# A scan of 256 steps: one tangent per stream's step, 64 features per product, and the other products laid between the steps

## The chip, the cores and the metric

The kernel runs on one core of one Trainium2 chip. The metric is the device time of one launch in microseconds (us); lower is better. Engines are called as the profile calls them: PE is the matrix engine, PEld its loading of weights, ACT, DVE and POOL are the other three computing engines, SP issues transfers.

## The reference, cut to what matters

The whole kernel is a stack of eight layers over 8 sequences of 256 tokens with 128 features (four attention-like layers and four feed-forward layers with experts). The change touches only the first layer, a recurrence over time with 16 heads of 8 features and 64 states each:

```python
x = tokens * rsqrt(mean(tokens**2) + 1e-4) * norm_w      # then (B, T, 16, 8)
a_t = tanh(a)                                            # (16, 64, 64)
def step(state, x_t):                                    # state (B, 16, 64)
    state = tanh(einsum('bhs,hst->bht', state, a_t) + einsum('bhd,hds->bhs', x_t, b))
    mixed = einsum('bhs,hsd->bhd', state, c) + skip[None] * x_t
    return (state, mixed)
_, outs = scan(step, zeros, moveaxis(x, 1, 0))           # 256 steps, one after the other
return tokens + outs @ w_out.T + b_out
```

Every step needs the state of the step before it. All arithmetic is in 32-bit floats.

## The kernel before

**What comes around the scan.** `tile_post_ln_blocks` first runs `l0_attn`: it loads the weights, normalizes the tokens in four groups, transposes them (L128), writes the scaled features `xd` (L205) and `xnT` (L209), runs the scan, and then multiplies by `w_out` (L280) and adds the residual. Only then do the experts of the first feed-forward layer (`experts`, L306, L301) and everything after it start; they need the scan's result. The order of instructions on each engine is chosen when the program is built, by a scheduler that goes by its own estimates of durations; a manual dependency can hold an order. A helper called `behind` adds such a dependency without a semaphore: it only says that one instruction is to stand after another.

**How states are laid out.** The 16 heads are two streams (`h` = 0, 1) of 8 heads. A stream has four stacks `k`; a stack holds two heads, one in partitions 0 to 63 and one in 64 to 127. In the free dimension of a state tile stand, for each step, the four stacks with two column groups `e` of 8 batches: 4 x 2 x 8 = 64 columns. Where the head of the upper 64 partitions is meant (`e` = 1), the lower partitions hold zeros in those columns, and the other way round; so one product with all 128 partitions as rows serves two heads. Which heads form a stack changes from even to odd steps, so that the product's two halves land in the right partitions for the next step.

**One step of one stream before.** Eight products (L239): for two pairs of stacks `s` and four column groups of 32 features `c`, each with 128 rows, 32 columns of weights from `a_sb` and 16 moving columns of the last state. They add to a bank of PSUM that already holds the input products. Then two tangents (L248), one for each half of the partitions, write the 64 x 32 results that are not zero to the state tile; the zeros are set once at the start (L188) and stay.

**A block.** `TB` is 16 steps. Before a block's steps, 64 input products (L224, 32 columns of weights, 128 moving columns: 8 steps of one parity) fill the two banks of the block; the pool has four banks, so that the next block's products may run while this block's steps go on. After a block, 16 output products (L259, 32 columns of weights, 128 moving columns) and four instructions on DVE (L269, L270) write `outsT`. Where these 64 and 16 products stand among the steps is decided by the scheduler: in the program before, the input products come in bunches of 2 to 28 in the first steps of a block, with none in most steps, and the output products in pairs around the block's end.

**A product in 32-bit floats** shows as two records of PE in the profile (8160 records for the 4080 products of L239), each with its own record on PEld. The array can be split by columns: products of 32 columns of weights use one of four column groups and run beside each other, products of 64 columns use one of two halves.

Of the kernel before, what the change touches and what calls it, by code (L numbers as in the profile page):

```python
# [42 lines left out]
def tile_post_ln_blocks(ctx: ExitStack, tc: tile.TileContext, I, out: bass.AP):  # L43
# [10 lines left out]
    def bank(pool):  # L54
        return pool.tile([P, 512], F32, tag=pool.name, name=pool.name)
# [103 lines left out]
    def l0_attn(x):  # L159

        TB = 16
        cols = [slice(32 * c, 32 * c + 32) for c in range(4)]
        low, high = slice(0, 64), slice(64, 128)
        with ExitStack() as es:
            wp = es.enter_context(tc.tile_pool(name="l0w", bufs=1))
            wk = es.enter_context(tc.tile_pool(name="l0k", bufs=2))
            a_sb = load(wp, "L0_a")  # L170
            b_sb = load(wp, "L0_b")
            c_sb = load(wp, "L0_c")
            normw = load(wp, "L0_norm_w")
# [36 lines left out]

            ps_m = es.enter_context(tc.tile_pool(name="ps_s", bufs=4, space=bass.MemoryType.PSUM))
            prev = [None, None]
            for blk in range(T // TB):
                ts = slice(blk * TB // 2, (blk + 1) * TB // 2)
                st = [states[h][blk % 2] for h in range(2)]
                us = [
                    bank(ps_m).rearrange("p (s u t e b) -> p s u t e b", s=2, u=2, t=TB // 2, e=2)
                    for h in range(2)
                ]
                for u in range(2):  # L220
                    for h in range(2):
                        for s in range(2):
                            for c in range(4):
                                PE.matmul(  # L224
                                    us[h][cols[c], s, u].rearrange("p t e b -> p t (e b)"),
                                    lhsT=b_sb[:, u, 4 * h + 2 * s + c // 2, 32 * (c % 2) : 32 * (c % 2) + 32],
                                    rhs=xd[:, ts, u, :, :].rearrange("p t e b -> p t (e b)"),
                                    start=(u == 0 and s == 0),
                                    stop=False,
                                    skip_group_check=True,  # L230
                                )
                for t in range(TB):
                    v, u = t // 2, t % 2
                    for h in range(2):
                        if prev[h] is not None:
                            for s in range(2):
                                for c in range(4):
                                    k = 2 * s + c // 2
                                    PE.matmul(  # L239
                                        us[h][cols[c], s, u, v].rearrange("p e b -> p (e b)"),  # L240
                                        lhsT=a_sb[:, u, 4 * h + k, 32 * (c % 2) : 32 * (c % 2) + 32],
                                        rhs=prev[h][:, k].rearrange("p e b -> p (e b)"),
                                        start=False,
                                        stop=(t == TB - 1),
                                        skip_group_check=True,
                                    )
                        for e, half in enumerate((low, high)):
                            S.activation(  # L248
                                st[h][half, v, u, :, e, :].rearrange("p (s k) b -> p s k b", s=2),
                                us[h][half, :, u, v, :, :],  # L250
                                AF.Tanh,
                            )
                        prev[h] = st[h][:, v, u]

                pm = bank(lanes[blk % 2].ps)[:, : TB * 2 * B].rearrange("p (u t e b) -> p u t e b", u=2, t=TB // 2, e=2)
                for u in range(2):
                    for k in range(2):
                        for q, c in enumerate(cols):
                            PE.matmul(  # L259
                                pm[c, u].rearrange("p t e b -> p t (e b)"),  # L260
                                lhsT=c_sb[:, u, 2 * q + k, :],
                                rhs=st[q // 2][:, :, u, 2 * (q % 2) + k].rearrange("p t e b -> p t (e b)"),
                                start=(u == 0 and k == 0),
                                stop=(u == 1 and k == 1),
                                skip_group_check=True,
                            )
                for u in range(2):
                    o = outsT[:, :, blk * TB : (blk + 1) * TB].rearrange("p b (t u) -> p t u b", u=2)[:, :, u]
                    V.scalar_tensor_tensor(o, xnT[:, ts, u], skip, pm[:, u, :, 0], ALU.mult, ALU.add)  # L269
                    V.tensor_tensor(o, pm[:, u, :, 1], o, ALU.add)  # L270

            for g in range(NG):
                xb = wk.tile([P, 4, D], F32, tag="sq", name="xb")
                V.scalar_tensor_tensor(
                    xb, x[g], 2.0, bout.unsqueeze(1).to_broadcast([P, 4, D]), ALU.mult, ALU.add
                )
                ps = quarters(bank(lanes[g % 2].ps))
                for j in range(4):
                    i = 4 * g + j
                    PE.matmul(  # L280
                        ps[:, j, :],
                        lhsT=outsT[:, i // 2, (i % 2) * P : (i % 2) * P + P],
                        rhs=woT,
                        start=True,
                        stop=True,
                    )
                V.tensor_tensor(xb, ps, xb, ALU.add)
                mixed(lanes[g % 2], g, xb)
# [1097 lines left out]
```

## Time and profile before

| | |
|---|---|
| median of 5 runs | 2153.83 us (2146.22 to 2169.53) |
| the profiled execution | 2153.46 us, of which the span of instructions is 2151.7 us |
| PE busy in the span | 1804.5 us (84%) |
| ACT busy | 949.4 us (44%) |
| first input product (L224) | 25.48 us from the span's start |
| last tangent (L248) | ends at 307.8 us |
| granted TensorE clock from 25.48 to 308.10 us | 0.69 of full speed on average |
| granted clock from 310 to 900 us | 0.96 |

Read it as a chain of stages. The scan takes 282 us of 2151.7 us, one eighth, and nothing else of weight runs beside it. In the profile's rows a form such as "128*32 128x16" is a product with 128 rows and 32 columns of weights and 128 x 16 of moving data. The duration of a record on PE runs from its start to the arrival of its last result; records follow each other more closely than that, since the array is a pipeline.

### The profile page before, as it was taken

The numbers are of one execution on the slowest core, as the hardware profiler recorded it, in microseconds if no ns is written. First come the engines' busy times: TensorE is split into PE (matmuls) and PEld (weight loads), VectorE is DVE, ScalarE is ACT, GpSimd is POOL, SyncE is SP. The second block draws the span as 40 slices with busy tenths as digits, with TensorE's granted clock in tenths as the row PEclk, the third lists the DMA queues.
The fourth block names the chain that finished last, engine by engine and source line by source line (L and its number), as shares of the span: only waits on it lengthen the run. The fifth ranks groups of instructions, "written<-read, shape, count | busy, mean of one in ns | idle before, by whom it ended". The sixth has DMA issues, their size and how long they took to land.

```text
span 2151.7 us, 46517 instructions
## 1 busy us (share of the span) xinstructions
PE 1804.5 (84%) x18200; PEld 1194.5 (56%) x18200; DVE 1266.6 (59%) x4476; ACT 949.4 (44%) x2385; POOL 290.7 (14%) x307
## 2 busy tenths in 40 slices
PE   5888878997899999999699753677967889998897
PEld 4666664455455544654367542555645666655564
DVE  3000025686887765689456842665668897557753
ACT  5767654472464426632333310233523554444413
POOL 1000000000000000004711077711065000000000
PEclk8666669998999999999789955788977999979958
DMA  3000007840232442226389795686721000000000
GB/s 93 5 5 5 5 4 238 245 142 0 79 93 69 113 122 81 67 86 177 95 294 314 219 295 170 216 309 208 208 60 38 1 1 1 1 5 6 1 1 11
DMA packets 186523, 219.66 MB, mean 102 GB/s; under 512 B 52896, under 2 KB 132256, under 8 KB 186304
## 3 DMA queue, kind: packets, MB, share of 16 engines
q1 hardware_dynamic: 163136, 164.24, 25.5%
q0 software_dynamic: 12800, 33.57, 5.0%
q10 hardware_dynamic: 10368, 18.88, 2.4%
q8 instruction: 143, 2.34, 0.4%
q14 instruction: 76, 0.62, 0.1%
HBM read 152.07 MB, written 64.55 MB: 101 GB/s over the span
## 4 chain that ended last, share of the span: by engine, by line
PE 61%; DVE 12%; ACT 9%; DMA 8%; POOL 5%; issue 4%; SPq 0%; ACTq 0%; POOLq 0%; DVEq 0%
PE ps_o L301 8%; PE ps_m L306 7%; ACT st L248 5%; PE ps_m L311 5%; PE ps_s L239 4%; PE ps L128 4%; PE ps L1002 3%; POOL got L586 3%; POOL placed L484 3%; PE ps L996 3%; DMA got<-made,pl 2%; PE ps_o L575 2%; PE ps L1122 2%; PE ps_s L224 2%; PE ps L1076 1%
## 5 line engine op out<-in xcount | busy, mean ns | idle before, releaser
L248 ACT ACTIVATE st<-ps_s 64x32 f32<-64x32 f32 x1024 | 195.7, 191 | 86.1 <-PE ps_s L239 50.0
L239 PE MATMUL ps_s<-st,L_a 128*32 128x16 f32 x8160 | 199.4, 206 | 40.8 <-ACT st L248 19.9
L308 ACT ACTIVATE h<-ps_m 128x512 f32<-128x512 f32 x196 | 116.0, 597 | 243.3 <-PE ps_m L306 226.8
L301 PE MATMUL ps_o<-h,wd 128*128 128x512 f32 x384 | 199.4, 604 | 7.9 <-DVE h L314 7.9
L239 PEld LDWEIGHTS ps_s<-st,L_a 128*32 128x32 f32 x8160 | 156.8, 134 | 86.2 <-ACT st L248 72.7
L306 PE MATMUL ps_m<-xT,wg 128*128 128x512 f32 x384 | 197.7, 598 | 7.5 <-ACT h L308 7.5
L455 POOL DMA_INDIRECT got<-in_F_w_dram,ei x32 | 30.7, 958 | 1113.7 <-DVE ei L442 964.0
L269 DVE SCALAR_TENSOR_TENSOR outsT<-xnT,L_skip,ps 128x64 f32<-128x64 f32 x32 | 10.4, 325 | 264.6 <-PE ps L259 184.3
L314 DVE TENSOR_TENSOR h<-h,bc 128x512 f32<-128x512 f32 x192 | 131.3, 686 | 46.4 <-ACT h L308 39.2
L484 POOL DMA_INDIRECT placed<-x,pl x128 | 126.4, 987 | 119.3 <-DVE pl L480 80.9
L586 POOL DMA_INDIRECT got<-made,pl x128 | 122.9, 960 | 126.6 <-DMA made<-ob 87.8
L311 PE MATMUL ps_m<-xT,wu 128*128 128x512 f32 x256 | 134.9, 609 | 4.7 <-ACT h L308 3.7
L575 PE MATMUL ps_o<-w,h 64*64 64x128 f32 x1152 | 96.4, 315 | 45.9 <-DVE h L570 35.5
L301 PEld LDWEIGHTS ps_o<-h,wd 128*128 128x128 f32 x384 | 72.7, 193 | 94.0 <-issue 63.5
L306 PEld LDWEIGHTS ps_m<-xT,wg 128*128 128x128 f32 x384 | 71.2, 191 | 91.6 <-issue 65.5
L312 DVE TENSOR_TENSOR h<-h,ps_m 128x512 f32<-128x512 f32 x132 | 89.9, 681 | 50.0 <-PE ps_m L311 45.2
L575 PEld LDWEIGHTS ps_o<-w,h 64*64 64x64 f32 x1152 | 75.6, 156 | 64.6 <-DVE h L570 47.8
L996 PE MATMUL ps<-nT,A_w 128*128 128x512 f32 x192 | 99.8, 634 | 8.4 <-DVE hT L998 5.6
L1002 PE MATMUL ps<-A_w,hT 128*128 128x128 f32 x768 | 99.4, 284 | 3.6 <-DVE hT L998 3.6
L577 ACT COPY ob<-ps_o 128x512 f32<-128x512 f32 x72 | 42.1, 585 | 136.7 <-PE ps_o L575 133.1
L1002 PEld LDWEIGHTS ps<-A_w,hT 128*128 128x128 f32 x768 | 93.8, 197 | 15.5 <-DVE hT L998 7.8
L565 PE MATMUL ps_m<-xg,w 128*64 128x64 f32 x1152 | 58.7, 254 | 39.2 <-DMA w<-further 16.9
(356 smaller groups left out, 3633.6 us busy)
## 6 DMA issues: line engine op xcount, KB each, us to landing
bc<-comb SPq DMA_DIRECT2D x128, 256.0 KB
placed<-zero SPq DMA_DIRECT2D x72, 256.0 KB
xb<-placed SPq DMA_DIRECT2D x72, 256.0 KB
made<-ob ACTq DMA_DIRECT2D x72, 256.0 KB
further<-got SPq DMA_DIRECT2D x32, 512.0 KB
w<-in_F_wg_dram SPq DMA_DIRECT2D x40, 256.0 KB
w<-in_F_wd_dram SPq DMA_DIRECT2D x40, 256.0 KB
bc<-comb SPq DMA_DIRECT2D x16, 512.0 KB
```

Of the source, the lines that this page charges most:

```text
L239: PE.matmul(us[h][cols[c], s, u, v].rearrange("p e b -> p (e b)"), lhsT=a_sb[:, u, 4 * h + k, 32 * (c % 2) : 32 * (c % 2) + 32], rhs=prev[ ...
L248: S.activation(st[h][half, v, u, :, e, :].rearrange("p (s k) b -> p s k b", s=2), us[h][half, :, u, v, :, :], AF.Tanh,)
L301: PE.matmul(acc[g], lhsT=w, rhs=h, start=begin, stop=end, skip_group_check=True)
L306: PE.matmul(pg, lhsT=wg, rhs=xT[g], start=True, stop=True)
L308: gate = S.activation(h, pg, func).ins
L311: PE.matmul(pu, lhsT=wu, rhs=xT[g], start=True, stop=True)
L314: V.tensor_tensor(h, h, bc[:, i * GT : (i + 1) * GT], ALU.mult)
L484: i = G.indirect_dma_start(placed[h][:, :], bass.IndirectOffsetOnAxis(rw[:, j, c : c + 1], 0), x[g][:, j, :], None).ins
L575: PE.matmul(po[k, i // 2, :], lhsT=h[k, i // 2, :], rhs=wd[k, i // 2, :], start=True, stop=True)
L586: G.indirect_dma_start(got[:, c, :], None, made[g // 2][:, :], bass.IndirectOffsetOnAxis(row[g][:, j, c : c + 1], 0))
L996: PE.matmul(ph, lhsT=w1[:, f * P : (f + 1) * P], rhs=nT, start=True, stop=True)
L1002: PE.matmul(po[:, j, :], lhsT=hT[:, f, j * P : (j + 1) * P], rhs=w2[:, f, :], start=(f == 0), stop=(f == 3),)
```

## The change

The state tile becomes flat: for every step 4 stacks x 2 `e` x 2 `z` x 8 columns = 128 columns, where `z` = 1 holds states and `z` = 0 holds zeros that are never overwritten, and 8 more zeros at the end. A tangent writes only the `z` = 1 columns, for all 128 partitions. A product reads 32 adjacent columns that start 8 columns earlier or later according to its half `c`, so that it meets states and zeros in the pattern that it needs. With that:

- a stream's step has four products with 64 columns of weights and 32 moving columns (before: eight with 32 and 16), and one tangent of 128 x 64 (before: two of 64 x 32);
- an input product has 64 columns of weights and 64 moving columns, and fills 8 steps instead of 16; 16 of them are done before the first step, and from then on exactly one stands behind each stream's step;
- the 16 output products of a block keep their 32 columns of weights and 128 moving columns; one stands behind every step of the second stream in the next block;
- the first step also multiplies by the state, which is zero;
- the two memsets of POOL and of DVE that clear the state tiles cover 2056 columns each instead of 1024.

```diff
-        low, high = slice(0, 64), slice(64, 128)
+        sides = [slice(0, 64), slice(64, 128)]
...
-                    t = wp.tile([P, TB // 2, 2, 4, 2, B], F32, tag=f"st{h}{k}", name=f"st{h}{k}")
+                    t = wp.tile([P, TB * 4 * 32 + 8], F32, tag=f"st{h}{k}", name=f"st{h}{k}")
...
-                us = [
-                    bank(ps_m).rearrange("p (s u t e b) -> p s u t e b", s=2, u=2, t=TB // 2, e=2)
-                for u in range(2):
-                    for h in range(2):
-                        for s in range(2):
-                            for c in range(4):
-                                PE.matmul(
-                                    us[h][cols[c], s, u].rearrange("p t e b -> p t (e b)"),
-                                    lhsT=b_sb[:, u, 4 * h + 2 * s + c // 2, 32 * (c % 2) : 32 * (c % 2) + 32],
-                                    rhs=xd[:, ts, u, :, :].rearrange("p t e b -> p t (e b)"),
...
+            HB = TB // 2
+            def inputs(n):
+                us = [
+                    bank(ps_m).rearrange("p (t u s e f b) -> p t u s e f b", t=HB // 2, u=2, s=2, e=2, f=2)
+                    for h in range(2)
+                ]
+                def product(u, h, s, c):
+                    return PE.matmul(
+                        us[h][sides[c], :, u, s, :, c, :],
+                        lhsT=b_sb[:, u, 4 * h + 2 * s + c, :],
+                        rhs=xd[:, n // 2 : (n + HB) // 2, u, :, :],
...
+            def outputs(blk):
+                def product(u, k, q):
+                    return PE.matmul(
+                        pm[cols[q], u],
+                        lhsT=c_sb[:, u, 2 * q + k, :],
+                        rhs=st[q // 2][:, :, u, 2 * (q % 2) + k, :, 1, :],
...
+            us, todo = inputs(0)
+            for f in todo:
+                f()
+            for n in range(T):
+                t, blk = n % TB, n // TB
+                if t == 0 and blk:
+                    outs, finish = outputs(blk - 1)
+                if n % HB == 0:
+                    now, ins = us, []
+                    if n + HB < T:
+                        us, ins = inputs(n + HB)
+                for h in range(2):
+                    for s in range(2):
+                        for c in range(2):
+                            k = 2 * s + c
+                            last = PE.matmul(
+                                now[h][sides[c], n % HB // 2, n % 2, s].rearrange("p e f b -> p (e f b)"),
+                                lhsT=a_sb[:, n % 2, 4 * h + k, :],
+                                rhs=prev[h][:, 32 * k + 8 * (1 - c) : 32 * k + 8 * (1 - c) + 32],
...
+                    S.activation(
+                        st[:, t * 128 : t * 128 + 128].rearrange("p (k e z b) -> p k e z b", k=4, e=2, z=2)[:, :, :, 1],
+                        now[h][:, n % HB // 2, n % 2].rearrange("p s e f b -> p (s e) f b"),
+                        AF.Tanh,
+                    )
+                    prev[h] = st[:, t * 128 : t * 128 + 136]
+                    more = [ins.pop(0)] if ins else []
+                    if h == 1 and outs:
+                        more.append(outs.pop(0))
+                    for f in more:
+                        behind(f().ins, last, "between two steps")
+                    if finish and not outs:
+                        finish()
+                        finish = None
+            outs, finish = outputs(T // TB - 1)
+            for f in outs:
+                f()
+            finish()
```

The instructions that `finish` issues are the four of DVE as before. Nothing outside `l0_attn` is edited.

More of the change, by code (lines that the diff above doesn't have):

```diff
@@ L211, in l0_attn @@
             ps_m = es.enter_context(tc.tile_pool(name="ps_s", bufs=4, space=bass.MemoryType.PSUM))
[L212 to L215, printed above, removed]
+            HB = TB // 2
+            def inputs(n):
                 us = [
-                    bank(ps_m).rearrange("p (s u t e b) -> p s u t e b", s=2, u=2, t=TB // 2, e=2)
+                    bank(ps_m).rearrange("p (t u s e f b) -> p t u s e f b", t=HB // 2, u=2, s=2, e=2, f=2)
@@ L218, in l0_attn @@
                     for h in range(2)
                 ]
-                for u in range(2):
-                    for h in range(2):
-                        for s in range(2):
-                            for c in range(4):
-                                PE.matmul(
-                                    us[h][cols[c], s, u].rearrange("p t e b -> p t (e b)"),
-                                    lhsT=b_sb[:, u, 4 * h + 2 * s + c // 2, 32 * (c % 2) : 32 * (c % 2) + 32],
-                                    rhs=xd[:, ts, u, :, :].rearrange("p t e b -> p t (e b)"),
[L228 to L264, printed above, removed]
-                                skip_group_check=True,
-                            )
@@ L267, in l0_attn @@
[L267 to L270, printed above, removed]
+                def product(u, h, s, c):
[3 more added lines that the diff above has]
+                        rhs=xd[:, n // 2 : (n + HB) // 2, u, :, :],
+                        start=(u == 0 and s == 0),
+                        stop=False,
+                        skip_group_check=True,
+                    )
@@ new lines, in inputs, with finish @@
+                todo = [
+                    (lambda a=(u, h, s, c): product(*a))
+                    for u in range(2) for h in range(2) for s in range(2) for c in range(2)
+                ]
+                return us, todo
+            def outputs(blk):
+                st = [states[h][blk % 2][:, : TB * 4 * 32] for h in range(2)]
+                st = [t.rearrange("p (t u k e z b) -> p t u k e z b", t=TB // 2, u=2, k=4, e=2, z=2) for t in st]
+                pm = bank(lanes[blk % 2].ps)[:, : TB * 2 * B].rearrange(
+                    "p (u t e b) -> p u t e b", u=2, t=TB // 2, e=2
+                )
+                ts = slice(blk * TB // 2, (blk + 1) * TB // 2)
+                def product(u, k, q):
[3 more added lines that the diff above has]
+                        rhs=st[q // 2][:, :, u, 2 * (q % 2) + k, :, 1, :],
+                        start=(u == 0 and k == 0),
+                        stop=(u == 1 and k == 1),
+                        skip_group_check=True,
+                    )
+                def finish():
+                    for u in range(2):
+                        o = outsT[:, :, blk * TB : (blk + 1) * TB].rearrange("p b (t u) -> p t u b", u=2)[:, :, u]
+                        V.scalar_tensor_tensor(o, xnT[:, ts, u], skip, pm[:, u, :, 0], ALU.mult, ALU.add)
+                        V.tensor_tensor(o, pm[:, u, :, 1], o, ALU.add)
+                return [
+                    (lambda a=(u, k, q): product(*a)) for u in range(2) for k in range(2) for q in range(4)
+                ], finish
@@ new lines, in l0_attn @@
+            us, todo = inputs(0)
+            for f in todo:
+                f()
+            outs, finish = [], None
+            prev = [states[h][1][:, (TB - 1) * 128 :] for h in range(2)]
+            for n in range(T):
[14 more added lines that the diff above has]
+                                rhs=prev[h][:, 32 * k + 8 * (1 - c) : 32 * k + 8 * (1 - c) + 32],
+                                start=False,
+                                stop=(n % HB == HB - 1),
+                                skip_group_check=True,
+                            ).ins
+                    st = states[h][blk % 2]
+                    S.activation(
+                        st[:, t * 128 : t * 128 + 128].rearrange("p (k e z b) -> p k e z b", k=4, e=2, z=2)[:, :, :, 1],
+                        now[h][:, n % HB // 2, n % 2].rearrange("p s e f b -> p (s e) f b"),
+                        AF.Tanh,
+                    )
+                    prev[h] = st[:, t * 128 : t * 128 + 136]
[7 more added lines that the diff above has]
+                        finish = None
```

## The prediction

> **What bounds the kernel now.** I read the page first, then the waits, the timeline and the table by stretches inside the scan.
>
> ```profile
> span 2151.7 us, 46517 instructions
> ...
> L248 ACT ACTIVATE st<-ps_s 64x32 f32<-64x32 f32 x1024 | 195.7, 191 | 86.1 <-PE ps_s L239 50.0
> L239 PE MATMUL ps_s<-st,L_a 128*32 128x16 f32 x8160 | 199.4, 206 | 40.8 <-ACT st L248 19.9
> ```
>
> Each of the two waits for the other: a recurrence, bound by the round trip of a stream, not by an engine. The timeline of steps without other products shows the round:
>
> ```profile
> 106.80 0.85 PE L239 MATMUL ps_s<-st,L_a 128*32 128x16 f32 x32 [0.15 <-ACT st L248]
> 107.34 0.84 ACT L248 ACTIVATE st<-ps_s 64x32 f32<-64x32 f32 x4 [0.16 <-PE ps_s L239]
> 107.80 0.85 PE L239 MATMUL ps_s<-st,L_a 128*32 128x16 f32 x32 [0.15 <-ACT st L248]
> ```
>
> One step of both streams takes 1.00 us here. For one stream: two tangents in a row 0.41 (2 x 0.192 and 0.02 between), 0.05 until PE's first weights, 0.41 for the eight products, 0.13 from the last result to the next tangent. The table by stretches says why it is 0.91 at other places (PE in the timeline restarts at 101.98 and 102.89):
>
> ```profile
> 45.60:52.42 6.82, 5.18 (x270) 4.18 (x261) 0.98 (x4) 4.87 (x26) 0.00 (x0) 1.00 0.02 5
> 52.43:62.66 10.23, 9.33 (x351) 7.58 (x347) 0.00 (x0) 7.36 (x39) 0.00 (x0) 0.50 0.02 5
> 25.48:308.10 282.62, 241.12 (x9693) 193.45 (x9696) 17.18 (x61) 196.18 (x1026) 0.00 (x0) 0.69 0.02 5
> ```
>
> The third number from the end is the granted clock: full for 6.8 us around a bunch of input products, half for 10.2 us of bare steps, in every block. At full clock the eight products take 0.32 instead of 0.41. The scan costs 282.6 us / 256 = 1.10 us a step: bare steps of 0.91 to 1.00, and the rest for 64 + 16 products a block.
>
> **What the clock follows.** I took every record's start, let a moving column stream for 0.83 ns at full clock and 1.67 at half (input products of 128 columns follow each other in one column group every 107 to 109 and 213 ns), and worked out for each 3.41 us, the spacing of the clock's changes, the share of time in which anything streams (products of fewer than 128 rows in proportion), times the clock. In the scan's 84 windows, up to 0.360 is followed by half clock, 0.372 or more by full; the same bound fits 534 of 535 windows up to 1850 us. So PE busy at 90% does not keep the clock; streaming does. Section "Part 1: The HAM clock gate" of the Trainium skill's "TensorE: Matmul & The Clock Gate" says that half clock returns after an idle window of some 3.4 us. There is no idle window in the scan, so by that sentence the clock would never fall here; the rows above show otherwise, and I go by them.
>
> **The change, part by part.** The memsets are 0.94 us longer each on POOL, which squares the tokens next. Behind that ACT waits 1.96 us for L_norm_d and DVE 1.95 us for L_b_out anyway: 0 to +1.9 us, I take 0. No transfer moves, on no queue.
>
> The tangents: 512 instead of 1024. 512 columns take 597 ns (L308), 256 take 383, so 0.84 ns a column: 0.192 + 32 x 0.84 = 0.22 us, against 0.41 for two. That is -0.19 on the round.
>
> The products of a step: the nearest rows have 64 columns of weights (L565) and, for the loading alone, 8 moving columns (L610):
>
> ```profile
> 1104.64 0.69 PE L565 MATMUL ps_m<-xg,w 128*64 128x64 f32 x16 [0.70 <-DMA w<-in_F_wg_dram]
> 326.78 0.96 PE L610 MATMUL ps<-F_router,xT 128*128 128x8 f32 x8
> ```
>
> L565: 16 records in two halves, so (0.69 - 0.22) / 8 = 0.058 between records of one half. L610: about 0.112 between records that stream only 8 columns, so 128 columns of weights set that pace and 64 set about 0.057. A step's four records per half therefore start at 0, 0.107 (the first load isn't hidden; L565's first spacing), 0.165 and 0.223; the other half 0.008 later; the last lasts 0.196 (0.183 for 16 columns, 0.222 for 64). That is 0.43 us where eight narrow products took 0.32. The bare round at full clock: 0.22 + 0.05 + 0.43 + 0.13 = 0.83, against 0.91.
>
> The input product behind each stream's step occupies one half for two records, 0.117. The round of 0.83 has room for both streams' 0.28 and both products, so the first 16 steps, which have no output products, take 0.84 each.
>
> The output products: each needs column groups of 32 between products of 64. Where the trace changes the form of the array, PE doesn't overlap:
>
> ```profile
> 1106.86 0.69 PE L873 MATMUL ps<-qT,kT 32*128 32x256 f32 x2
> 1107.40 0.38 PE L874 MATMUL ps<-qT,kT 32*128 32x128 f32 x2
> 1107.71 0.70 PE L861 MATMUL ps<-A_tri,zb 128*128 128x256 f32 x2
> 1108.24 0.38 PE L862 MATMUL ps<-A_tri,zb 128*128 128x128 f32 x2
> ...
> 1098.45 1.09 PE L575 MATMUL ps_o<-w,h 64*64 64x128 f32 x16
> 1099.47 0.68 PE L565 MATMUL ps_m<-xg,w 128*64 128x64 f32 x14
> ```
>
> Same form: the next starts 0.15 to 0.17 before the last one ends. Other form: 0.07 before its end, and its weights load only then. The order of the changed program is, for every step from 16 on: stream A's four products, its input product, B's four, its input product, one output product; two changes of form a step, 240 times. Laid out at full clock, from A's first record: A 0 to 0.231; its input product at 0.281 and 0.340 in one half; B in that half at 0.398 to 0.573, in the other from 0.29 if it may start ahead; B's input product there, last at about 0.581, done at 0.803; output product at 0.733 and, 0.024 + 0.109 on, at 0.868, done (0.273) at 1.141; A again at 1.071. If B may not start ahead, everything behind it is 0.117 later: 1.19. In the before trace, records of L239 start at 47.35 in free column groups while L224, which stands ahead of them, still waits until 47.45 in others, so I take a value near the lower end, 1.08. Both streams are ready earlier than that (0.83 after their own start): the round no longer binds, PE's queue does. Behind the output product stands the next step of both streams, so this is all on the path. Its own waits, for DVE's release of the bank, are met (DVE waits 184.3 us for PE L259, not PE for DVE).
>
> The Trainium skill's "TensorEngine Tiling (Array Packing)", section "Tiling Modes", speaks against this change: changing the tiling mode, as opposed to the tile, drains the array. Taken as a wait for the full end, 0.07 later than the rows at both changes, it would make the step 0.14 longer, 34 us over the scan, and the kernel slower.
>
> The sum, on the profiled 2153.5 us (span 2151.7; the median is 2153.8): first input product at 25.5 as before; 16 of them, 8 a half x 2 records x 0.107, 1.8 at half clock; 16 steps, the first three at half clock (1.17), 14.5; 240 steps x 1.08 = 259.2, less 1 for the last 8 without input products. Last tangent 300.0, against 307.8; the end behind it is alike (16 output products, four on DVE). So -7.8 us: 2146 us. The steps' bounds 1.07 and 1.19 give -10 and +19. The rest of the program is the same work, but the scheduler has ordered it a little differently in some 80 places; that is worth perhaps 8 us either way.
>
> **The rivals.**
> 1. *The clock stays at half.* At half clock the same layout of a bare step with its input products takes 1.17 us, of which something streams for 0.82 (0.91 less overlaps), a share of 0.70: times 0.5 that is 0.35, under the bound of 0.372; with output products 2.0 us and 0.31. At full clock it is 0.55 to 0.6, which holds. So there are two stable speeds, and only the opening bunch (1.75 us of pure streaming) can lift the first: by my sum, if a window begins between 0.4 us before it and 1.2 after, half of all positions. For it: 0.35 lies under the bound. Against it: a gap of 0.02 is within my layout's error, and windows vary. If it decides: 27.3 + 18.7 + 480 = 526, +218 us: 2372.
> 2. *No wait between halves and quarters.* The trace has no change from 64 to 32 columns with all rows alike. Without the wait the round binds again, 0.85 a step: last tangent at 245.8, -62 us: 2091.
> 3. *Strict order in PE's queue*, 1.19 a step: 2173. For it: two input products in one half may fill that half's queue.
> That the change doesn't do what it says is no rival: the changed program's listing shows one product behind each step.
>
> **How the numbers follow.** Forecast 0.57 (its own range 2122 to 2172), clock at half 0.19, no wait 0.13, strict order 0.11. The range 2088 to 2200 leaves out the slow clock only. A measurement can tell about 1%, 21.5 us. Faster by more: 0.13 and 0.18 of the forecast's, 0.31. Slower: 0.19, half of strict order and a little of the forecast's lower half, 0.28. Within: 0.41.
>
> **What would show it.** After: granted clock 1.00 from about 30 us to the scan's end; 0.83 to 0.85 us a step in the first block, 1.05 to 1.12 after; each output product's first record 0.07 before the end of B's input product; tangents of 0.22 us with idle time ended by PE. Wrong if the clock is 0.50 in the scan, or if steps from 16 on take as long as those before.

## The result, and the profile after

The changed kernel takes 2151.26 us (median; 2140.26 to 2170.08), the kernel before in the same series 2147.49 us (2132.59 to 2169.53): a ratio of 1.0015, 95% interval 1.0005 to 1.0026. It is slower by 3 to 4 us, about 0.15%. The forecast, 2146 us, was 8 us faster than its base; the direction was wrong.

A correction first: the section on the kernel before says that a block has 64 input products. It has 32 (L224: 512 products, 16 blocks). The prediction names the 64 once more, but no term of its sum uses it.

The page of the profiled execution after. Its rows of groups read: busy time and mean ns of one, then idle time before and what ended it.

```profile
span 2145.1 us, 37878 instructions
...
PEclk9999998998999999999899965787978998989958
...
L288 PE MATMUL ps_s<-st,L_a 128*64 128x32 f32 x4096 | 196.4, 226 | 0.0
...
L297 ACT ACTIVATE st<-ps_s 128x64 f32<-128x64 f32 x512 | 114.2, 223 | 167.3 <-PE ps_s L288 136.2
...
L224 PE MATMUL ps_s<-xd,L_b 128*64 128x64 f32 x1024 | 150.4, 239 | 3.9 <-ACT xd L207 3.9
```

The tangents cost 114 us instead of 196, 0.223 us each as forecast. The first five slices of PEclk are full, where in the kernel before the clock changed between full and half in them. And yet ACT's idle time before the tangents has doubled, from 86 to 167 us, 136 of it ended by PE, while PE has none before its own products. The round trip no longer sets the pace; PE does.

The table by stretches, of the first block and of later ones (busy time of PE, PEld, DVE, ACT and POOL with their records, then clock, DMA share, GB/s):

```profile
31.00:41.00 10.00, 10.00 (x271) 9.93 (x269) 0.00 (x0) 5.95 (x28) 0.00 (x0) 1.00 0.01 4
100.00:200.00 100.00, 100.00 (x1975) 76.01 (x1973) 5.49 (x20) 39.95 (x180) 0.00 (x0) 1.00 0.01 3
```

Both at full clock. In the first 28 tangents fit into 10 us, in the second 180 into 100 us. A step is 0.783 us in block 0, which has no output products, and 1.115 us in each of the blocks 2 to 14. The last tangent ends at 308.7 us, before at 307.8.

The timeline of one step of PE says why (start, duration, line, records):

```profile
100.04 0.41 PE L250 MATMUL ps<-st,L_c 128*32 128x128 f32 x2
100.37 0.42 PE L288 MATMUL ps_s<-st,L_a 128*64 128x32 f32 x8
100.63 0.25 PE L224 MATMUL ps_s<-xd,L_b 128*64 128x64 f32 x1
100.63 0.30 PE L288 MATMUL ps_s<-st,L_a 128*64 128x32 f32 x2
100.71 0.22 PE L224 MATMUL ps_s<-xd,L_b 128*64 128x64 f32 x1
100.77 0.31 PE L288 MATMUL ps_s<-st,L_a 128*64 128x32 f32 x5
100.91 0.25 PE L224 MATMUL ps_s<-xd,L_b 128*64 128x64 f32 x1
100.92 0.22 PE L288 MATMUL ps_s<-st,L_a 128*64 128x32 f32 x1
101.00 0.22 PE L224 MATMUL ps_s<-xd,L_b 128*64 128x64 f32 x1
101.15 0.41 PE L250 MATMUL ps<-st,L_c 128*32 128x128 f32 x2
101.49 0.42 PE L288 MATMUL ps_s<-st,L_a 128*64 128x32 f32 x8
```

Stream A's products start at 100.37, its input product at 100.63 and 100.71. Stream B's first two records go out beside them at 100.63 and 100.71, in the free half; its other six records, by their spacing two of them in the free half, only from 100.77 on, although that half had room. So B's input product comes at 100.91 and 101.00 and ends at 101.22 (101.00 + 0.22). At 101.15, 0.07 before that end, the output product starts, and 0.07 before its own end A starts again at 101.49. Two changes of form a step, each as read from the trace of before.

### The profile page after: what moved, and what is told of

Read it like the earlier page. It is cut to its first block, busy times and chain, and to the rows that moved or that the text cites. A ratio compares the mean times of both kernels' runs of the same rounds, so it can differ in the third digit from the quotient of the medians.

```text
span 2145.1 us, 37878 instructions
## 1 busy us (share of the span) xinstructions
PE 1833.7 (85%) x14136; PEld 1212.1 (57%) x14136; DVE 1265.8 (59%) x4476; ACT 866.8 (40%) x1873; POOL 292.7 (14%) x307
## 4 chain that ended last, share of the span: by engine, by line
PE 64%; DMA 11%; DVE 9%; POOL 7%; issue 4%; ACT 4%; SPq 1%; POOLq 0%; ACTq 0%; DVEq 0%
PE ps_o L345 8%; PE ps_m L350 7%; PE ps_s L288 7%; PE ps_m L355 5%; POOL got L630 4%; PE ps L250 4%; PE ps L128 4%; PE ps L1046 3%; POOL placed L528 3%; DMA got<-in_F_w_dram,ei 3%; PE ps L1040 3%; PE ps_s L224 3%; DMA further<-got 3%; DMA got<-made,pl 2%; PE ps L1150 2%
## 5 line engine op out<-in xcount | busy, mean ns | idle before, releaser
L288 PE MATMUL ps_s<-st,L_a 128*64 128x32 f32 x4096 | 196.4, 226 | 0.0
L288 PEld LDWEIGHTS ps_s<-st,L_a 128*64 128x64 f32 x4096 | 168.1, 137 | 47.6 <-ACT st L297 47.3
L297 ACT ACTIVATE st<-ps_s 128x64 f32<-128x64 f32 x512 | 114.2, 223 | 167.3 <-PE ps_s L288 136.2
L224 PE MATMUL ps_s<-xd,L_b 128*64 128x64 f32 x1024 | 150.4, 239 | 3.9 <-ACT xd L207 3.9
L224 PEld LDWEIGHTS ps_s<-xd,L_b 128*64 128x64 f32 x1024 | 99.7, 141 | 4.2 <-ACT xd L207 4.2
```

What stands on the lines that cost most here:

```text
L224: return PE.matmul(us[h][sides[c], :, u, s, :, c, :], lhsT=b_sb[:, u, 4 * h + 2 * s + c, :], rhs=xd[:, n // 2 : (n + HB) // 2, u, :, :], s ...
L288: last = PE.matmul(now[h][sides[c], n % HB // 2, n % 2, s].rearrange("p e f b -> p (e f b)"), lhsT=a_sb[:, n % 2, 4 * h + k, :], rhs=prev[ ...
```

## The experiments

They fell on three chips, where the kernel before takes 2328, 2334 and 2161 us itself. The scan is alike where it can be compared (a step of the changed form takes 1.115 us in the first series and in cold_start, a step of out64's form 0.83 to 0.85 us on all three chips); what differs lies behind it. So a step and the scan's end are compared as they are, times only as ratios to the kernel before on the same chip. Below, the wide form is the changed one, with 64 columns of weights in a step's products, and the narrow form the one before, with 32; a window is one of the 3.41 us between two possible changes of the clock.

| kernel | us a step, blocks 2 to 14 | last tangent ends | ratio to before (95%) |
|---|---|---|---|
| before | 1.07 to 1.16 | 307.8 | 1 |
| after | 1.115 | 308.7 | 1.0015 (1.0005 to 1.0026) |
| out64 | 0.833 | 241.4 | 0.982 (0.977 to 0.986) |
| out_by_four | 0.907 | 260.1 | 0.989 (0.985 to 0.992) |
| spread_only | 1.05 to 1.16 | 308.8 | 1.002 (0.9995 to 1.005) |
| cold_start | 1.115 | 317.6 | 1.000 (0.997 to 1.003) |
| inputs_after_b | 1.067 | 297.9 | two executions, see there |
| wide_bunched | 1.08 to 1.30 | 345.1 | 1.029 (1.023 to 1.035) |
| out64_order | 0.834, 0.846 | 245.3 | 0.975 (0.972 to 0.978) |
| out64_start | 0.834, 0.851 | 248.8 | 0.972 (0.969 to 0.975) |
| out64_start_b | 0.808, 0.826 | 249.4 | 0.973 (0.969 to 0.976) |
| wide_no_outputs | 0.809, 0.826 | not comparable | not comparable |
| narrow_no_outputs | 1.00 to 1.15 | not comparable | not comparable |

Two numbers in a row are alternating blocks. My theory was that the two changes of form at every output product take what the shorter round and the full clock give; the rivals were that the product itself takes it, whatever its form, or that the clock was not what the kernel before waited for.

### out64: the same output products without a change of form

```diff
-                        pm[cols[q], u],
+                        pm[sides[q // 2], u],
...
-                        start=(u == 0 and k == 0),
-                        stop=(u == 1 and k == 1),
+                        start=(u == 0 and k == 0 and q % 2 == 0),
+                        stop=(u == 1 and k == 1 and q % 2 == 1),
...
-    zc = np.zeros((2, 64, 2, 8, 4, 8), f)
+    zc = np.zeros((2, 64, 2, 8, 8, 8), f)
...
-                zc[e, :, 1 - u, i, h % 4, :] = a["L0_attn_c"][h]
+                zc[e, :, 1 - u, i, 4 * (i // 2 % 2) + h % 4, :] = a["L0_attn_c"][h]
```

> Output products get 64 columns of weights (half of them zeros) and use the halves like all the others; number, order and moving columns stay. Theory (each output product costs two changes of form): without them a step from 16 on needs only the passes of the fuller half, A 0.23, B 0.23, an input product 0.12, an output product 0.22, so 0.80 to 0.85 us against 1.115; the scan ends 65 to 75 us earlier, the kernel takes about 2080 us. Rival (the output product itself sits in PE's queue and costs its 0.3 us whatever its form): steps stay at 1.05 or more, gain under 15 us.

Measured 0.833 us a step; the scan ends at 241.4, 67 us earlier than in after. From its timeline:

```profile
150.40 0.22 PE L288 MATMUL ps_s<-st,L_a 128*64 128x32 f32 x1
150.46 0.30 PE L250 MATMUL ps<-st,L_c 128*64 128x128 f32 x1
150.48 0.22 PE L224 MATMUL ps_s<-xd,L_b 128*64 128x64 f32 x1
150.59 0.27 PE L250 MATMUL ps<-st,L_c 128*64 128x128 f32 x1
150.67 0.42 PE L288 MATMUL ps_s<-st,L_a 128*64 128x32 f32 x8
```

The output product starts at 150.46, before the second record of B's input product (150.48) has even gone out, and the next step's products start at 150.67 while it still runs. Nothing drains. The product is as long as before (0.30 and 0.27 us); its form was the price. The rival falls, and with it a wait for the banks that DVE frees: both are still there in out64. But the scan ends 66 us earlier than in the kernel before, and the kernel gained only 49 of them (2279.1 against 2328.5); out64_order asks where 17 went.

### out_by_four: fewer changes of form, the same products

```diff
-                    if h == 1 and outs:
-                        more.append(outs.pop(0))
+                    if h == 1 and outs and t % 4 == 0:
+                        more += [outs.pop(0) for _ in range(4)]
```

> The narrow output products stay, but four of them, one for each column group, stand behind every fourth step, so there are two changes of form in four steps instead of eight. Theory (changes of form cost, products do not): three steps of 0.77 to 0.80 and one of 1.12 to 1.2 in four, 0.88 on average, the scan ends about 55 us earlier. Rival (each output product costs its own 0.3 us): four of them at one place cost as much as four at four places, no change within 10 us.

0.907 us a step: a quarter of the changes, and 0.208 of the 0.28 us between after and out64 are gone, three quarters. The time goes with the changes, not with the number of products. It can be the products' own length as well, since four of them in four column groups run side by side:

```profile
100.10 0.43 PE L250 MATMUL ps<-st,L_c 128*32 128x128 f32 x8
```

Eight records take 0.43 us here, two take 0.41 in after; that a product of this length costs little without the change is shown by out64 alone. Here too some 16 of 48 us of scan are missing in the total.

### wide_no_outputs and narrow_no_outputs: the price of a product

```diff
-                        V.scalar_tensor_tensor(o, xnT[:, ts, u], skip, pm[:, u, :, 0], ALU.mult, ALU.add)
-                        V.tensor_tensor(o, pm[:, u, :, 1], o, ALU.add)
+                        V.tensor_scalar(o, xnT[:, ts, u], skip, None, ALU.mult)
...
-                return [
-                    (lambda a=(u, k, q): product(*a)) for u in range(2) for k in range(2) for q in range(4)
-                ], finish
+                return [], finish
```

> After without the 16 output products of each block (the products with L_c are left out, so this part of the layer's result is missing): no change of form in the scan. Theory: all steps as the first block's, 0.77 to 0.80 us, scan end at about 231 us; the price of one output product with its two changes of form is then 1.115 - 0.78 = 0.33 us, against 0.05 in out64. Rival (a step from 16 on is slower for another reason, such as the waits on the banks that DVE frees): steps stay over 1.0 us.

> spread_only without the output products (left out as in wide_no_outputs): what stays is the kernel before with one input product behind each stream's step, at full clock. Theory from spread_only's timeline (an input product of 128 columns holds one column group for 0.22 us, and the next stream's products in that group wait; ACT is busy 0.87 of the 1.10 us): 1.0 to 1.05 us a step, the output product adds 0.05 to 0.1. Rival (the output products make the difference between 0.91 and 1.10): 0.91 to 0.95 us a step, scan end at about 265 us.

Without the output products the layers behind the scan need not wait for it and move into its first blocks; only the later steps are read. The wide form takes 0.818 us (mean of the two), a little more than expected. So an output product with two changes of form costs 1.115 - 0.818 = 0.30 us, and one in the form of its neighbours 0.833 - 0.818 = 0.015. That it costs so little has a condition, as a line of wide_no_outputs shows:

```profile
100.04 0.48 PE L266 MATMUL ps_s<-st,L_a 128*64 128x32 f32 x9 [0.18 <-ACT st L275]
```

Without output products PE waits for a tangent before this step's products, 0.18 us, so the padded product has room. The narrow form takes 1.00 to 1.15, mean 1.06: see the next run.

### spread_only: the spreading alone, in the form of before

```diff
+                    for u in range(2) for h in range(2) for s in range(2) for c in range(4)
...
                     more = [ins.pop(0)] if ins else []
                     if h == 1 and outs:
                         more.append(outs.pop(0))
                     for f in more:
-                        behind(f().ins, last, "between two steps")
+                        i = f().ins
+                        if last is not None:
+                            behind(i, last, "between two steps")
```

(This is part of the difference from after; the steps, tangents and states are those of the kernel before.)

> The kernel before (two tangents, eight products of 32 columns a stream's step) with one thing changed: one input product stands behind each stream's step and one output product behind each step of the second stream. Theory (before, the bunches let the clock fall to half between them; spread products keep it up, and with one form there is no change of form): granted clock 1.00 through the scan, 0.91 us a step, the scan ends about 45 us earlier than before. Rival (the clock is not what a step before waits for, and added products stand in the queue): 1.0 to 1.1 us a step, no gain against before.

The clock did what was expected, the steps did not:

```profile
100.00:200.00 100.00, 87.87 (x3493) 59.18 (x3494) 5.48 (x20) 69.98 (x366) 0.00 (x0) 1.00 0.02 5
```

Full clock throughout, and still 366 tangents in 100 us, four a step: 1.09 us. The scan ends at 308.8, as before. The timeline shows a step that is held up:

```profile
100.25 0.26 PE L280 MATMUL ps_s<-st,L_a 128*32 128x16 f32 x9
100.35 0.27 PE L220 MATMUL ps_s<-xd,L_b 128*32 128x128 f32 x1
100.46 0.25 PE L280 MATMUL ps_s<-st,L_a 128*32 128x16 f32 x9
...
101.03 0.32 PE L280 MATMUL ps_s<-st,L_a 128*32 128x16 f32 x16
101.19 0.39 PE L220 MATMUL ps_s<-xd,L_b 128*32 128x128 f32 x2
```

At 101.03 a stream's 16 records go out in one piece of 0.32 us. At 100.25 the second stream's come in parts: the last of them start only at 100.46 and later, behind the two records of the input product (100.24 and 100.35) that holds their column group. Its tangents start that much later. Without the output products (narrow_no_outputs) the step is still 1.06, against 0.91 for bare steps at full clock: the input products take 0.15 of it, the output products 0.05. So spread products cost what the clock gives. The rival was right here: full clock that is had by spreading brings nothing in the narrow form. That the waiting for the column group is the cause is read from the timeline, no run took it away.

### wide_bunched: the new form without the spreading

```diff
-                    more = [ins.pop(0)] if ins else []
-                    if h == 1 and outs:
-                        more.append(outs.pop(0))
+                    more = []
+                    if h == 1:
+                        more, ins = ins, []
+                        more, outs = more + outs, []
```

and the first products of the next step are ordered behind the bunch.

> After, with the input products in one bunch of 16 behind every eighth step and the output products in one bunch of 16 behind the first step of the next block; the tangents and the step's products stay as wide as in after. Two changes of form a block instead of 32. By the streaming rule a bare step at full clock streams in 0.28 of 0.76 us, a share of 0.37, at the bound: theory A (the rule): the clock falls to half between bunches and the step is 0.95 to 1.0 us there, 1.0 to 1.1 us a step with the bunches, scan about as long as after. Theory B (only the changes of form and the queue matter, the clock holds): 0.77 us for a bare step and some 3 us a block for the bunches, 0.96 a step, the scan ends about 38 us earlier.

```profile
185.90:189.30 3.40, 2.92 (x74) 2.48 (x72) 0.69 (x3) 1.80 (x8) 0.00 (x0) 1.00 0.00 0
189.30:196.10 6.80, 6.70 (x118) 6.30 (x115) 0.00 (x0) 2.36 (x11) 0.00 (x0) 0.50 0.01 2
```

From 73 us to 346 every stretch at full clock lasts one window of 3.4 us: eight tangents in 3.4 us, then 11 in 6.8 at half clock. The clock is 0.62 between 100 and 200 us, a step up to 1.30, the scan 37 us longer than before, the kernel 2.9% slower. Theory A's mechanism holds, its size was too small: a bare step at half clock is 1.03 us (tangents of one stream at 174.27, 175.29, 176.32), and the bunches are mostly at half clock too, 1.75 us for 16 input products and 1.9 for 16 output products, where I had counted them nearer to full. The spreading is what keeps the wide form at full clock. Of the 68 us in the total, 37 are the scan and some 14 the order of the last layer (see out64_order); 17 I can't place.

### cold_start and out64_start_b: can the clock stay at half?

cold_start lets PE stand idle before the first step:

```diff
+            S.activation(xd_zero, xd.rearrange("p t u e b -> p (t u e b)")[:, -136:], AF.Copy, scale=0.0)
+            for h in range(2):
+                for r in range(20):
+                    S.copy(states[h][1][:, (TB - 1) * 128 :], xd_zero)
```

> After, with 41 instructions on ACT between the opening products and the first step, some 12 us in which PE does nothing, so that the steps begin at half clock. By the prediction's rule (share of time that streams, times the clock, 0.35 against a bound of 0.372) the clock stays at half: scan at 1.17 and 2.0 us a step, about 2372 + 12 us. Rival (the steps of the changed kernel stream enough to lift the clock by themselves): the clock is full within two or three windows of 3.41 us, about 12 to 15 us over the changed kernel.

```profile
41.23 0.22 ACT L302 ACTIVATE st<-ps_s 128x64 f32<-128x64 f32 x1 [0.31 <-PE ps_s L293]
41.77 0.22 ACT L302 ACTIVATE st<-ps_s 128x64 f32<-128x64 f32 x1 [0.31 <-PE ps_s L293]
42.30 0.22 ACT L302 ACTIVATE st<-ps_s 128x64 f32<-128x64 f32 x1 [0.31 <-PE ps_s L293]
42.71 0.56 ACT L302 ACTIVATE st<-ps_s 128x64 f32<-128x64 f32 x2 [0.19 <-PE ps_s L293]
43.45 0.56 ACT L302 ACTIVATE st<-ps_s 128x64 f32<-128x64 f32 x2 [0.19 <-PE ps_s L293]
```

Tangents follow each other every 0.53 us, a step of 1.07 at half clock; at 42.4 the clock turns full and a step is 0.75. PE stood idle for 7.2 us, the scan ends 9 us later than in after. The steps lift the clock by themselves, the prediction's first rival does not happen. (The total does not show these 9 us: its ratio to before is 1.000, after's 1.0015. No run shows why.) But not because its rule is wrong. By the way of counting laid down in the prediction, the window before streams for 0.69 of its time (times 0.5: 0.345, the clock stays), the next for 0.81 (0.405, it rises). The rival's layout, 1.17 us a step at half clock and a share of 0.70, was too slow; the steps take 1.07.

out64_start_b (its edit is below) has the state itself, by accident. Its steps of block 0 at half clock, as PE's timeline and the groups of the stretch 34 to 48 us show them (ns: least, median, most):

```profile
40.47 0.46 PE L228 MATMUL ps_s<-xd,L_b 128*64 128x64 f32 x4
40.72 1.01 PE L292 MATMUL ps_s<-st,L_a 128*64 128x32 f32 x16
41.54 0.46 PE L228 MATMUL ps_s<-xd,L_b 128*64 128x64 f32 x4
...
L292 PE MATMUL ps_s<-st,L_a x214: 261/294/294, 33.7 to 47.8; 128*64 128x32 f32 x107
```

A step takes 1.07 us again and its records the 294 ns of half clock (223 at full), but A and B overlap more in this order, so something streams for only 0.65 to 0.67 of the time: 0.33. For six windows, until the output products of the next block raise it to 0.93, the clock stays at half. (The trace's first record of the clock is full clock from 54.6 us on; before it the lengths of PE's records tell the clock.) Block 0 of inputs_after_b (the next run) has the same products in the same order and no output products either, but there the clock was full from 30.7 us on:

```profile
35.41 0.75 PE L288 MATMUL ps_s<-st,L_a 128*64 128x32 f32 x16
35.99 0.31 PE L224 MATMUL ps_s<-xd,L_b 128*64 128x64 f32 x4
36.16 0.74 PE L288 MATMUL ps_s<-st,L_a 128*64 128x32 f32 x16
```

A step takes 0.75 us, something streams for 0.51 to 0.53 of the time, and the clock stays full. Two stable speeds of one loop, as the prediction's rival had it; the rival needs an order that overlaps more than the changed kernel's. By the same counting the start decides which of the two it is: the window that holds the opening products streams for 0.80 of its time in inputs_after_b (times 0.5: 0.40) and, as it falls otherwise, for 0.66 in out64_start_b (0.33).

### inputs_after_b: does the queue explain the 0.035 us?

```diff
-                    more = [ins.pop(0)] if ins else []
+                    more = [ins.pop(0), ins.pop(0)] if ins and h == 1 else []
```

> After, with both input products of a step behind stream B's products (one in each half) instead of one behind each stream; the order A, input, B, input, output becomes A, B, input, input, output, still with two changes of form a step. Theory (the 0.035 us that a step took above the forecast are B's later products and its input product waiting in PE's queue for the half that A's input product holds): B starts in both halves at once, the two input products run side by side, 1.03 to 1.07 us a step against 1.115, the scan ends 10 to 20 us earlier. Rival (the changes of form take longer than 0.07 us each before the end of the last, wherever the input products stand): 1.11 us a step, no change.

```profile
150.04 0.41 PE L250 MATMUL ps<-st,L_c 128*32 128x128 f32 x2
150.37 0.66 PE L288 MATMUL ps_s<-st,L_a 128*64 128x32 f32 x16
150.86 0.31 PE L224 MATMUL ps_s<-xd,L_b 128*64 128x64 f32 x4
151.10 0.41 PE L250 MATMUL ps<-st,L_c 128*32 128x128 f32 x2
```

A's and B's 16 records now go in one piece, the two input products side by side, and the step is 1.067 us; the scan ends at 297.9, 10.8 us earlier than after. The waiting was B's, for the half that A's input product held; the rival falls. Of this kernel only two executions can be compared, 2320.9 and 2325.6 us against 2333.8 for before, so its total has no interval.

### out64_order and out64_start: what out64 gave back, and the start

Between the last product with A_wqv and the end of the span, out64, out_by_four and wide_bunched take 147 to 150 us, before, after and the others 133 to 137 (but for wide_no_outputs, whose layers stand in an order of their own: 151). The scheduler, which goes by its own estimates, had written the last layer in another order for these three. A memset that moves from POOL to DVE is enough to give out64 the order of after:

```diff
-                    (V if h else G).memset(t, 0.0)
+                    (V if h or k else G).memset(t, 0.0)
```

> As out64, and one of POOL's two memsets moves to DVE, so that the scheduler writes the last layer's instructions in the order that after has; in out64 and out_by_four they stood in another order, and their last layers took 30 us longer than in the other runs of the same chip. Theory (that order gave back part of out64's gain): the scan ends 67 us earlier than before as in out64, and the kernel is 65 us faster than before, ratio about 0.970 instead of 0.982. Rival (the end is slower because the scan is shorter, by transfers or the clock): ratio 0.982 again, last layer as long as in out64. Beside it the theory for the start: with one memset less on POOL the first input product begins 0.5 to 1 us earlier than in after (26.7 us).

The groups with A_wqv of out64 and of out64_order; the number before the semicolon is the start of the last one:

```profile
L981 PE MATMUL ps<-A_wqv,nT x192: 379/379/796, 1450.9 to 2127.6; 128*128 128x256 f32 x192
...
L981 PE MATMUL ps<-A_wqv,nT x192: 379/379/796, 1464.9 to 2134.0; 128*128 128x256 f32 x192
```

From there to the ends of their spans, 2275.0 and 2267.6, it is 147.4 and 133.6 us. The scan ends 62.5 us before that of before, and the kernel is 59 us faster (0.975 of 2333.8): nearly all of the scan's gain arrives. So the order of the last layer, not the shorter scan, gave back most of the 17 us. (The 30 us for the last layer in that expectation was mis-read from unlike stretches; 14 is the difference.)

The part on the start failed: the first input product began at 27.9 us, not earlier than after's 26.7. DVE now cleared three tiles and its first sum over the squares came at 7.7 us. The next try left both engines free for the first squares:

```diff
-                    (V if h else G).memset(t, 0.0)
+                    if (h, k) not in [(0, 0), (0, 1), (1, 0), (1, 1)]:
+                        G.memset(t, 0.0)
...
-                G.tensor_tensor(out=sq, in0=x[g], in1=x[g], op=ALU.mult)
+                square = G.tensor_tensor(out=sq, in0=x[g], in1=x[g], op=ALU.mult).ins
+                if g == 2:
+                    for h, k in [(0, 0), (0, 1), (1, 0), (1, 1)]:
+                        behind(G.memset(states[h][k], 0.0).ins, square, "squares first")
```

> As out64, with all four memsets of the state tiles on POOL behind the third of its four squarings; the last layer's instructions stand in the order of after. Theory for the start (in after POOL's two memsets, 0.86 us longer each, delay the first squaring from 3.5 to 5.1 us, and the first input product from 25.5 to 26.7): squaring at about 3.5 us, first input product at 25.0 to 25.6. Scan as in out64, 215 us, ends at about 241: 67 us before the kernel before, ratio about 0.970. Rival for the start (the first input product waits for a transfer, whatever POOL does): 26 to 28 us.

POOL's timeline of before, of after and of out64_start:

```profile
3.52 2.04 POOL L192 TENSOR_TENSOR sq<-x 128x512 f32<-128x512 f32 x2 [0.15 <-DMA x<-in_x_dram]
6.31 2.04 POOL L192 TENSOR_TENSOR sq<-x 128x512 f32<-128x512 f32 x2 [0.75 <-DMA x<-in_x_dram]
```

```profile
5.07 3.02 POOL L194 TENSOR_TENSOR sq<-x 128x512 f32<-128x512 f32 x3
8.79 1.04 POOL L194 TENSOR_TENSOR sq<-x 128x512 f32<-128x512 f32 x1 [0.70 <-DVE rs_i L93]
```

```profile
7.44 7.10 POOL L198 MEMSET st<- 128x2056 f32 x4
14.52 1.03 POOL L195 TENSOR_TENSOR sq<-x 128x512 f32<-128x512 f32 x1
```

In after the first squaring starts 1.55 us later than before, as the memsets make it. In out64_start 7.1 us of memsets stand ahead of the fourth squaring, it ends at 15.6 instead of 9.8, and the first input product comes at 30.7, 4.0 us later than in after. Neither of the two starts expected was hit, and both misses say the same: the way from the squares to the first input product has little slack (1.7 us in out64_start: 5.7 later, 4.0 come through), and what is put ahead of a squaring or of its sum delays the scan. This kernel, out64_start_b and out64_order are the fastest of those measured, at 0.972, 0.973 and 0.975 of before.

out64_start_b adds the edit of inputs_after_b to out64_start:

> out64_start with the order of inputs_after_b (both input products behind stream B). If a step of 0.833 us is still bound by PE's queue (the fuller half's passes: 0.80), evening out the halves gives 0.79 to 0.81 us a step, the scan ends 5 to 10 us earlier than in out64_start. If it is bound by the round trip of a stream, as the prediction's second rival has it (0.85), no change within 2 us.

0.817 us a step against 0.843: PE's queue was still the bound, by a little more than 0.025 us. That is worth 5.4 us over the blocks 2 to 15; half clock in the blocks 0 and 1 cost 5.3 and the start came 0.8 later, so the scan ends 0.6 us later than in out64_start, and the totals are alike (0.9723 and 0.9725).

## Why the prediction was wrong, step by step

**What bounds the kernel before, and the clock.** That the round trip set the pace holds for bare steps, and so does that the clock made the difference of 0.91 to 1.00 in them; what the bunches had hidden is that the other products, when spread in the narrow form, cost more than this difference (spread_only). The forecast did not rest on that.

**The clock after.** "Granted clock 1.00 from about 30 us to the scan's end" came true: it is full from 30.7 to 317.4 us. In all the scans run here, windows with a share times clock of up to 0.345 were followed by half clock and windows from 0.39 on by full clock; in between both occur (0.355 rose, 0.38 fell). The prediction's bound of 0.360 to 0.372 is the middle of a blurred zone, not an edge: of the windows of the kernel before up to 1850 us some 525 of 533 lie on its right side (the prediction has 534 of 535), the others between 0.355 and 0.40. The first rival, with a chance of 0.19, fell with its layout, not with its rule. The Trainium skill's "TensorE: Matmul & The Clock Gate", "Part 1: The HAM clock gate", ties half clock to an idle window; in wide_bunched the clock falls with PE 2.92 of 3.40 us busy and no idle window, so the measurement decides against it here.

**Tangent and first 16 steps.** 0.223 us as forecast. Block 0 took 0.783 a step, forecast 0.84: a stream's first two records of a half stand 0.079 us apart, not 0.107. From the first step's first product to the first tangent of block 1 that is 13.2 us against 14.5.

**The mode change.** The mechanism stands: 0.07 us before the end of the last, twice a step, 240 times. The Trainium skill's "TensorEngine Tiling (Array Packing)", "Tiling Modes", says that a change of mode drains the array, without a price. The prediction, from its rows, had put 34 us on a wait for the full end, 0.07 later at each change; the trace of after starts the other form 0.07 us before the modelled end, so that addition did not come. That the change itself is dear is right, 0.30 us for a product with two of them.

**The step that failed: "240 steps x 1.08".** It is 1.115. The prediction's layout let all of B's records in the free half run ahead while B's others waited for A's input product, and closed at 1.071. In the trace only the first two ran ahead; the rest, and with them B's input product (0.54 and 0.63 us after A's first record instead of 0.52 and 0.58), came later. The truth lies between the forecast and the "strict order" rival (1.19), and the prediction chose "near the lower end" by one row of the narrow form, where four column groups stand open instead of two halves. inputs_after_b takes the wait away and lands at 1.067, the layout's own number. The term was 8.8 us short over the 240 steps (267.0 instead of 258.2).

**The memsets.** Bounded at 0 to +1.9 us, taken as 0, measured +1.2. The cover that the prediction named, ACT's wait for L_norm_d, is not there: that transfer landed at 15.8 instead of 16.3 us, and ACT then waited 0.55 us for DVE.

**The sum.** +1.2 for the start, -1.3 for block 0, +8.8 for the rest: the last tangent at 308.7 instead of 300.0. The first two cancel by chance. Against before it is +0.9, and the measured difference of the medians is 3.8. The other 3 us must lie behind the scan; the interval of the ratio leaves room for 0 to 5, and the two traces do not show where they are. They are within the 8 that the prediction allowed for the scheduler's order; out64 shows that this allowance was too small, some 14 us in one case.

**The second rival**, no wait between halves and quarters, does not happen, but its price was nearly right: with no change of form a step is 0.833 and the scan ends 66 us earlier (out64), where the rival had 0.85 and 62. Its reason, that the round trip then binds, is not what fits: out64_start_b shows that PE's queue still did, so the near hit is in part luck.

## What to carry to other kernels

Before small products are laid between a recurrence's steps, compare their form of the array with their neighbours': 240 output products of 32 columns among products of 64 cost 0.30 us each and took all that the rest of the change had given, while the same products padded with zeros to 64 columns cost 0.015, in a loop where PE had some room. A gain at one place is read at that place first (the last tangent), and then at the end: the scheduler may write a far layer in another order and take a quarter of it back.

## What was not expected

- The clock has two stable speeds in one and the same loop: 1.07 us a step at half for six windows (block 0 of out64_start_b), 0.75 at full (block 0 of inputs_after_b).
- Spreading the other products brought the narrow scan to full clock (1.00 instead of 0.69 on average) and did not speed it up at all: the same 282 us.
- An output product padded to twice its columns with zeros costs next to nothing here: 0.015 us.
- One memset of 1.8 us on another engine decides, through the scheduler, over 14 us at the far end of the program.
